# Fourth neighbour by SyncE or TensorE, and one in 42 history runs fetched by SyncE, in a recommender kernel

## The chip, the cores and the metric

The kernel runs on one core of a Trainium2 chip. The metric is the device time of one execution, in microseconds. The engines are named as in the profile: PE is TensorE, PEld its weight loads, DVE is VectorE, ACT is ScalarE, POOL is GpSimd and SP is SyncE. A letter q behind a name (SPq, ACTq) means the engine's sequencer, which runs register loads, waits and DMA issues.

## The reference

There are 50,001 items. Each has a row of 32 numbers in `E_in`, one in `E_out`, one of 64 numbers in `E_hist` and `E_tgt`, and a list of 32 neighbouring items. There are 16,384 users, each with 100 history items and one target item.

```python
def _neighbor_attn(E, near_full):            # for E_in (a_sus) and E_out (a_inf)
    V = E[near_full]                         # 32 neighbour rows per item
    scores = einsum('nd,nkd->nk', E, V) / sqrt(32)
    w = softmax(scores, axis=-1)
    return einsum('nk,nkd->nd', w, V)
h = concat([E_hist[history], a_sus[history], a_inf[history]])   # 100 rows of 128 per user
t = concat([E_tgt[target],  a_inf[target],  a_sus[target]])     # 1 row of 128 per user
x = h * t[:, None, :]
z = relu(x @ W1.T + b1)
scores = z @ W2[0]
exp_A = exp(scores) * ((history != target[:, None]) & (history != 0))
attn = exp_A / sum(exp_A) ** 0.5
s = sum(h * attn[..., None])                 # one number over all users
# then a cosine-like quotient of s and t per user, and a sigmoid
```

The cost is in two gathers of rows at random places: 32 neighbour rows for each item, then 100 item rows for each user.

## The kernel before

**Item stage.** The items are padded and cut into 23 blocks of 17 sub-blocks of 128 items, one item to a partition: 391 sub-blocks `s`. For each, a tile `v` of 128 x 32 x 64 numbers is filled with the neighbours' rows (`E_in` and `E_out` side by side, 256 bytes a row) from the input `egeo`. The 32 neighbours of a sub-block are fetched in three ways:

- Most by POOL: one indirect DMA (`nc.gpsimd.indirect_dma_start`, L215) fetches one neighbour of all 128 items.
- The last three (`NAUX` = 3) by ACT and DVE, with no DMA. `transposed` (L165 to L184) first puts the whole of `egeo` into SBUF, turned round, as `geoT`: one column of 128 numbers holds the rows of two items. `columns` (L222) loads 32 column addresses into an engine's registers (L189) and copies 32 single columns into a tile `g` (L229). `AUX` says which engine copies which quarter of which neighbour: six blocks of 32 on ACT and six on DVE. `turn` (L231) turns the `g` tiles back by TensorE, `even` (L238) writes the even item of each pair into `v`, and `odd_half` (L245) overwrites it where the odd one is wanted.
- The fourth last, in two of three sub-blocks (`SPNUM, SPDEN = 2, 3`), by SP: 128 single DMAs of 256 bytes from addresses in registers (L210), 32 addresses to one register load. In the third sub-block POOL fetches it.

The rest of an item is `products`, `scores`, `largest`, `exponents`, `weighted`, `attend`, `attended` and `finish`, on DVE and ACT. `finish` copies the result into two row buffers, `row` and `trow`, that ACT writes to the DRAM tensors `table` and `ttab` once in 17 sub-blocks. The order on PE, ACT, DVE and SP is written out by hand in the loop over `s` (L345 to L396): the stages of `s`, `s - 1`, `s - 2` and `s - 3` are interleaved. `v` has five buffers, so POOL and SP may be up to five sub-blocks ahead of the last reader of `v`. Ahead of the loop all 66 chunks of `geoT` are made at one go (L340).

**User stage.** The users are cut into 128 chunks `c` of 128, one user to a partition. The 100 history positions of a chunk make 13 groups `g`: twelve of eight positions and one of four. `gather` (L468) fetches each position of a group by one indirect DMA of POOL from `table` (L475, 512 bytes a row) into a tile `h`, of which there are six. `turn` (L484) transposes the eight 128 x 128 blocks (L490), multiplies by the target (L492) and sums rows (L495). `hidden` is the matrix product (L510) and relu (L511), `scored` the second product, one column per position (L519). `target_rows` (L429) fetches the target rows of a chunk with one more indirect DMA and, for every fourth chunk, has SP load the history numbers `hidx` (L433). The order within each engine is the scheduler's here.

A short last stage makes the sum over users and the output.

Of the kernel before, what the change touches and what calls it, by code (L numbers as in the profile page):

```python
# [18 lines left out]
P = 128  # L19
# [18 lines left out]
AUX = ("AAAA", "AADD", "DDDD",)  # L38
NAUX = len(AUX)
SPNUM, SPDEN = 2, 3  # L40
ENGINE = {"A": E.Activation, "D": E.DVE}
# [9 lines left out]
NG = L // LG  # L51


@with_exitstack
def kernel(
# [57 lines left out]
    with (  # L113
# [8 lines left out]
        tc.tile_pool(name="n_pt", bufs=3, space=bass.MemoryType.PSUM) as n_pt,  # L122
    ):
# [4 lines left out]
        def load(it):  # L128
# [4 lines left out]
            row = n_in.tile([P, NSUB, D], F32, name="row")  # L133
            nc.sync.dma_start(row[:, :, 0:DE], ehist_v[it])
            trow = n_in.tile([P, NSUB, 2 * G], F32, name="trow")
# [16 lines left out]
            nc.vector.tensor_copy(colf[:, :, 0:1], nidx[:, :, K - NAUX - 1 : K - NAUX])  # L152
# [10 lines left out]
            its[it] = (nidx, own, row, trow, odd, cols)  # L163

        def transposed(q):  # L165
# [10 lines left out]
            for n0 in range(0, n, 4):  # L176
                m = min(4, n - n0)
                ps = n_pt.tile([P, 4, P], F32, name="pt")
                for r in range(m):
                    nc.tensor.transpose(ps[:, r, 0:h], st[0:h, n0 + r, :], ident[0:h, 0:h])  # L180
                if (n0 // 4) % 2:
                    nc.vector.tensor_copy(into[:, n0 : n0 + m, :], ps[:, 0:m, 0:h])
                else:
                    nc.scalar.copy(into[:, n0 : n0 + m, :], ps[:, 0:m, 0:h])  # L184

        def registers(s, a, engine, i0, low, top):
# [3 lines left out]
                its[it][5][r : r + 1, i0 : i0 + NREG],  # L190
# [6 lines left out]

        def gather(s):
# [3 lines left out]
            g = [n_g.tile([P, P], F32, name=f"g{a}") for a in range(NAUX)]  # L202
            subs[s] = {"v": v, "g": g}
            k1 = K - NAUX - 1
            by_sp = s * SPNUM % SPDEN < SPNUM
            if by_sp:
# [7 lines left out]
            for k in range(k1 if by_sp else k1 + 1):  # L214
# [7 lines left out]
        def columns(s, a, i0):  # L222
# [3 lines left out]
            g = subs[s]["g"][a].bitcast(U8)  # L226
            copy = nc.scalar.copy if e == "A" else nc.vector.tensor_copy
            for i in range(i0, i0 + NREG):
                copy(g[:, 4 * i : 4 * i + 4], geoT_b[:, ds(vals[i - i0] - geoT_at, 4)])  # L229

        def turn(s):  # L231
            back = n_pt.tile([P, 4, P], F32, name="pt")
            for a in range(NAUX):
                nc.tensor.transpose(back[:, a, :], subs[s]["g"][a], ident)  # L234
            subs[s]["back"] = back
            subs[s]["aux"] = subs[s]["v"][:, K - NAUX : K].rearrange("p k t d -> p k (t d)")

        def even(s):  # L238
            it, j = divmod(s, NSUB)
            nc.scalar.copy(subs[s]["aux"], subs[s]["back"][:, 0:NAUX, 0 : 2 * G])  # L240
# [4 lines left out]
        def odd_half(s):  # L245
            it, j = divmod(s, NSUB)
            nc.vector.copy_predicated(
                subs[s]["aux"],
                its[it][4][:, j, :]
                .rearrange("p (a o) -> p a o", o=1)  # L250
                .to_broadcast([P, NAUX, 2 * G]),
                subs[s]["back"][:, 0:NAUX, 2 * G : 4 * G],
# [72 lines left out]
        def finish(s):  # L325
            it, j = divmod(s, NSUB)
            _, _, row, trow, _, _ = its[it]
            for t in range(2):
                nc.scalar.copy(
                    trow[:, j, t * G : (t + 1) * G], row[:, j, D - (t + 1) * G : D - t * G]  # L330
                )
            if j == NSUB - 1:
                nc.scalar.dma_start(table_v[it], row)
                nc.scalar.dma_start(ttab_v[it][:, :, DE:D], trow)
# [5 lines left out]
        for q in range(-(-PAIRS // (NST * P))):  # L340
            transposed(q)
        blocks = [(a, i0) for a in range(NAUX) for i0 in range(0, P, NREG)]
        acts = [(a, i0) for a, i0 in blocks if AUX[a][i0 // NREG] == "A"]
        dves = [(a, i0) for a, i0 in blocks if AUX[a][i0 // NREG] == "D"]
        for s in range(NT + 3):  # L345
            if s < NT:
                if s % NSUB == NSUB // 2 and s // NSUB + 1 < NITER:
                    load(s // NSUB + 1)
                gather(s)
# [3 lines left out]
            def act(i):  # L353
                if now and i < len(acts):
                    columns(s, *acts[i])

            def dve(i):
                if now and i < len(dves):
# [5 lines left out]
            if one:  # L364
                turn(s - 1)
# [269 lines left out]
```

## Time and profile before

| | |
|---|---|
| Time of the runs shown | 45,601.21 us median of 3 (45,563.7 to 45,709.14) |
| Profiled execution, its own time | 30,160.56 us |
| Span of the profile | 30,158.8 us |
| Item stage, first to last gather of POOL | 9.0 to 13,973.8 us |
| User stage, first to last gather of POOL | 14,001.6 to 30,140.0 us |
| Indirect DMAs by POOL | 11,078 (L215), 12,800 (L475), 128 (target rows) |
| Single-row DMAs by SP (L210) | 33,408 |
| Single-column copies by ACT and by DVE (L229) | 75,072 each |
| Mean granted PE clock | 0.799 (1.00 in the item stage, some 0.62 in the user stage) |

The profiled execution took about two thirds of the median of the timed runs. The profile does not show why.

How to read the page: part 1 gives the busy time of each engine. Part 2 cuts the span into 40 slices of 754 us, with one digit for the busy tenths of each. Part 4 follows the chain of work that ended last. Part 5 lists groups of instructions, with busy time and the mean ns of one, then the idle time ahead of them and what ended it. In the list of waits a line reads: who waited (engine, tile, line) <- for whom: total us, times, longest.

### The profile page before, as it was taken

To read this page: it belongs to the slowest core of one execution; us is meant where nothing else is said; L and a number is where in the kernel's file an instruction comes from. 1 tells how busy PE (TensorE), PEld (TensorE's weight loads), DVE (VectorE), ACT (ScalarE), POOL (GpSimd) and SP (SyncE) were. 2 spreads that over 40 slices of the span, in tenths; PEclk is the share of its full clock that TensorE was granted. 3 is DMA by queue.
4 is the path that set the end of the run, shared out by engine and by line. 5 is a ranking of instruction groups with operands and counts; after the bars stand their busy time and mean duration, and the time that the engine had idled before them with its cause. 6 is when DMAs were issued, how large, how long until landed. Compare 5 with 4: busy or idle time off the path is not lost.

```text
span 30158.8 us, 370867 instructions
## 1 busy us (share of the span) xinstructions
PE 13513.8 (45%) x46323; PEld 7666.4 (25%) x46323; DVE 13913.7 (46%) x83509; ACT 10305.2 (34%) x81987; POOL 22658.7 (75%) x24012
## 2 busy tenths in 40 slices
PE   1000000000000000003787787887887877878877
PEld 0000000000000000001444454444444444444444
DVE  5677777777777777775222222222222222222222
ACT  5565555555555555553111111111111111111111
POOL 6777777777777777777777777777777777777777
PEclk9999999999999999998656656666666666566566
DMA  2111111111111111111111111111111111111111
GB/s 62 31 36 32 32 34 34 32 32 34 34 32 32 34 34 32 32 34 40 54 53 54 53 54 53 54 53 54 53 54 53 54 53 54 53 54 53 54 53 52
DMA packets 1013118, 1347.05 MB, mean 45 GB/s; under 512 B 604800, under 2 KB 617664, under 8 KB 1007648
## 3 DMA queue, kind: packets, MB, share of 16 engines
q0 software_dynamic: 768192, 1211.79, 15.2%
q1 hardware_dynamic: 138480, 60.23, 0.8%
q10 hardware_dynamic: 103920, 51.31, 0.6%
q14 instruction: 2155, 17.65, 0.2%
q8 instruction: 371, 6.08, 0.1%
HBM read 1283.13 MB, written 51.30 MB: 44 GB/s over the span
## 4 chain that ended last, share of the span: by engine, by line
POOL 36%; issue 18%; DMA 16%; SPq 15%; PE 6%; DVE 4%; DVEq 0%; POOLq 0%; ACT 0%; ACTq 0%
POOL h L475 24%; DMA h<-table,hidx 13%; SPq L210 12%; POOL v L215 12%; PE z_ps L510 3%; SPq L189 3%; DMA v<-in_egeo_dram,nidx 2%; DVE g L229 1%; PE score L519 1%; PE hT_ps L490 1%; DVE xT L492 1%; DVE sc L268 0%; DVE prod L258 0%; DVEq L189 0%; DMA v<-in_egeo_dram 0%
## 5 line engine op out<-in xcount | busy, mean ns | idle before, releaser
L475 POOL DMA_INDIRECT h<-table,hidx x12800 | 12079.0, 944 | 3900.8 <-issue 3290.5
L215 POOL DMA_INDIRECT v<-in_egeo_dram,nidx x11078 | 10458.2, 944 | 3515.2 <-issue 3221.9
L229 ACT COPY g<-geoT 128x4 uint8 x75072 | 7377.3, 189 | 3385.9 <-issue 2729.6
L492 DVE TENSOR_TENSOR xT<-hT_ps,tT 128x1024 f32<-128x1024 f32 (+1 forms) x1664 | 1969.1, 1183 | 10939.1 <-PE hT_ps L490 10938.9
L511 ACT ACTIVATE z<-z_ps,b_sb 128x512 f32<-128x512 f32 x3200 | 2201.3, 688 | 12759.8 <-PE z_ps L510 12744.8
L490 PE MATMUL hT_ps<-ident,h 128*128 128x128 f32 x12800 | 5082.2, 414 | 3211.3 <-DMA h<-table,hidx 3001.2
L229 DVE COPY g<-geoT 128x4 uint8 x75072 | 5877.5, 197 | 808.2 <-issue 688.4
L234 PE MATMUL pt<-ident,g 128*128 128x128 f32 x1173 | 543.7, 471 | 12496.1 <-ACT g L229 10195.4
L510 PE MATMUL z_ps<-xT,w1T 128*128 128x512 f32 x6400 | 5806.6, 1009 | 24.7 <-DVE xT L492 24.6
L490 PEld LDWEIGHTS hT_ps<-ident,h 128*128 128x128 f32 x12800 | 2427.2, 193 | 8549.1 <-DMA h<-table,hidx 7900.2
L519 PEld LDWEIGHTS score<-w_sb,z 128*128 128x128 f32 x25600 | 4299.8, 253 | 0.6 <-issue 0.6
L519 PE MATMUL score<-w_sb,z 128*128 128x1 f32 x25600 | 3991.2, 278 | 0.0
L234 PEld LDWEIGHTS pt<-ident,g 128*128 128x128 f32 x1173 | 213.3, 184 | 12822.0 <-ACT g L229 10467.5
L258 DVE TENSOR_TENSOR prod<-v,own_ps 128x2048 f32<-128x2048 f32 x391 | 894.8, 2288 | 2684.3 <-DMA v<-in_egeo_dram 1470.5
L495 DVE TENSOR_REDUCE hsum<-h 128x8 f32<-128x1024 f32 (+1 forms) x1664 | 1943.4, 1168 | 0.0
L510 PEld LDWEIGHTS z_ps<-xT,w1T 128*128 128x128 f32 x6400 | 1886.8, 354 | 112.9 <-issue 70.3
L298 DVE TENSOR_TENSOR wv<-v,ex 128x1024 f32<-128x1024 f32 x782 | 1463.7, 1872 | 0.0
L268 DVE TENSOR_REDUCE sc<-prod 128x64 f32<-128x2048 f32 x391 | 889.7, 2275 | 0.0
L311 DVE TENSOR_REDUCE att<-wv 128x64 f32<-128x2048 f32 x391 | 883.7, 2260 | 0.1
L285 ACT ACTIVATE ex<-sc,top 128x32 f32<-128x32 f32 x782 | 227.0, 290 | 1343.5 <-DVE top L277 1330.8
L526 DVE TENSOR_TENSOR ea<-ea,keep 128x100 f32<-128x100 f32 x128 | 33.9, 265 | 1171.2 <-ACT ea L525 1171.2
L240 ACT COPY v<-pt 128x192 f32<-128x192 f32 x391 | 123.8, 317 | 1135.4 <-PE pt L234 1135.4
(67 smaller groups left out, 1585.7 us busy)
## 6 DMA issues: line engine op xcount, KB each, us to landing
v<-in_egeo_dram SPq DMA_DIRECT2D x33408, 0.2 KB
h<-table,hidx POOLq DMA_INDIRECT x12800
v<-in_egeo_dram,nidx POOLq DMA_INDIRECT x11078
table<-row ACTq DMA_DIRECT2D x23, 1088.0 KB
own<-in_egeo_dram SPq DMA_DIRECT2D x23, 544.0 KB
row<-in_ehist_dram SPq DMA_DIRECT2D x23, 544.0 KB
ttab<-trow ACTq DMA_DIRECT2D x23, 544.0 KB
ttab<-in_etgt_dram ACTq DMA_DIRECT2D x1, 12500.0 KB
```

The lines of the kernel that those rows point to most:

```text
L189: _, vals = nc.values_load_multi_w_load_instructions(its[it][5][r : r + 1, i0 : i0 + NREG], engines=[engine], min_val=low, max_val=top, sk ...
L210: nc.sync.dma_start(v[i0 + i : i0 + i + 1, k1].rearrange("p t d -> p (t d)").bitcast(U8), egeo_b[:, ds(vals[i], 8 * G)],)
L215: nc.gpsimd.indirect_dma_start(out=v[:, k].rearrange("p t d -> p (t d)"), out_offset=None, in_=egeo, in_offset=bass.IndirectOffsetOnAxis(a ...
L229: copy(g[:, 4 * i : 4 * i + 4], geoT_b[:, ds(vals[i - i0] - geoT_at, 4)])
L298: nc.vector.tensor_tensor(subs[s]["wv"][:, t].rearrange("p d k -> p k d"), subs[s]["v"][:, :, t, :], subs[s]["ex"][0][:, t, :] .rearrange( ...
L475: nc.gpsimd.indirect_dma_start(out=h[:, q, :], out_offset=None, in_=table, in_offset=bass.IndirectOffsetOnAxis(ap=u["hidx"][:, l : l + 1], ...
L490: nc.tensor.transpose(hT_ps[:, q, :], h[:, q, :], ident)
L492: x = nc.vector.tensor_tensor(xT[:, 0:w, :], hT_ps[:, 0:w, :], u["tT"].to_broadcast([D, w, P]), ALU.mult)
L495: s = nc.vector.tensor_reduce(u["hsum"][:, g * LW : g * LW + w], h[:, 0:w, :], AX.X, ALU.add)
L510: nc.tensor.matmul(z_ps, w1T, xT[:, q : q + LG, :], start=True, stop=True)
L511: nc.scalar.activation(z[:, q : q + LG, :], z_ps, AF.Relu, bias=b1_sb)
L519: nc.tensor.matmul(u["score"][:, l : l + 1], z[:, q, :], w2_sb, start=True, stop=True)
```

## The change

Item stage:

- `AUX` has a fourth entry ahead of the other three, "PPPP": four neighbours instead of three and two thirds are fetched without POOL, in every sub-block from the seventh on. `CYCLE = "PSSPS"` says who fetches the fourth: SP as before (S, 231 sub-blocks), or TensorE (P, 154). In a P sub-block `by_tensor` loads 128 addresses into PE's registers, 32 at a time, and makes 128 products of the identity with one column of `geoT`, which put the columns into a PSUM tile `pc` (one buffer). It runs in two halves of 64, one in the iteration before the sub-block's own and one in it. `evict` has ACT copy `pc` to SBUF, and `turn`, `even` and `odd_half` then treat four neighbours instead of three.
- The first six sub-blocks (`NFIRST`) have all 32 neighbours fetched by POOL. The 66 chunks of `geoT` are made during them, two at each of ACT's six places in an iteration, and all their evictions are by ACT.
- `trow` is gone. `row` is 160 numbers wide, one copy in `finish` repeats one half behind the other, and both DRAM writes read from it.

User stage:

- Of 768 runs of sixteen positions (two groups), every 42nd is fetched by SP: 18 runs. `one_by_one` has DVE make byte offsets `hoff`, and for each of 128 users SP loads 16 offsets into registers and issues 16 DMAs of 512 bytes into a tile `hs`, of which there are two. The first two runs are issued at the start of the stage, and run i + 2 where run i is used.
- The history numbers are loaded four blocks ahead (`AHEAD`), in `history_of`, from six buffers.

```diff
-AUX = ("AAAA", "AADD", "DDDD",)
+AUX = ("PPPP", "AAAA", "AADD", "DDDD")
-SPNUM, SPDEN = 2, 3
+CYCLE = "PSSPS"
+NFIRST = 6
+UG = 2
+UNIT = 42
+AHEAD = 4
...
+        tc.tile_pool(name="n_pc", bufs=1, space=bass.MemoryType.PSUM) as n_pc,
...
+        def kind(s):
+            return "" if s < NFIRST else CYCLE[s % len(CYCLE)]
...
-            by_sp = s * SPNUM % SPDEN < SPNUM
-            if by_sp:
+            if kind(s) == "S":
...
-            for k in range(k1 if by_sp else k1 + 1):
+            for k in range(k1 if kind(s) else K):
                 nc.gpsimd.indirect_dma_start(
...
             for i in range(i0, i0 + NREG):
-                copy(g[:, 4 * i : 4 * i + 4], geoT_b[:, ds(vals[i - i0] - geoT_at, 4)])
+                column = geoT_b[:, ds(vals[i - i0] - geoT_at, 4)]
+                if e == "P":
+                    nc.tensor.matmul(
+                        g[:, i : i + 1], ident, column.bitcast(F32), start=True, stop=True
+                    )
+                else:
+                    copy = nc.scalar.copy if e == "A" else nc.vector.tensor_copy
+                    copy(g.bitcast(U8)[:, 4 * i : 4 * i + 4], column)
+
+        def by_tensor(s, half):
+            if s >= NT or kind(s) != "P":
+                return
+            if half == 0:
+                subs[s] = {"g": [None] * NAUX}
+                subs[s]["g"][0] = n_pc.tile([P, P], F32, name="pc")
+            for i0 in range(half * P // 2, (half + 1) * P // 2, NREG):
+                columns(s, 0, i0)
+
+        def evict(s):
+            if kind(s) == "P":
+                g = n_g.tile([P, P], F32, name="g0")
+                nc.scalar.copy(g, subs[s]["g"][0])
+                subs[s]["g"][0] = g
...
             act(0)
             for i in range(5, len(dves)):
                 dve(i)
             if one:
+                evict(s - 1)
                 turn(s - 1)
                 even(s - 1)
                 odd_half(s - 1)
                 products(s - 1)
+            by_tensor(s, 1)
+            by_tensor(s + 1, 0)
             dve(0)
...
+        def one_by_one(c, g):
+            hs = u_hs.tile([P, UG * LW, D], F32, name="hs")
+            hoff = u_hs.tile([P, UG * LW], I32, name="hoff")
+            nc.vector.tensor_scalar(
+                hoff,
+                hists[c // BSUB][:, c % BSUB, g * LW : (g + UG) * LW],
+                9, None, ALU.logical_shift_left,
+            )
+            for p in range(P):
+                _, vals = nc.values_load_multi_w_load_instructions(
+                    hoff[p : p + 1, :], engines=[E.SP], min_val=0,
+                    max_val=(ITEMS - 1) * 4 * D,
+                    skip_runtime_bounds_check_because="worked out from an item's number",
+                )
+                for q in range(UG * LW):
+                    nc.sync.dma_start(
+                        hs[p : p + 1, q, :].bitcast(U8), table_b[:, ds(vals[q], 4 * D)]
+                    )
+            for i in range(UG):
+                early[c, g + i] = hs[:, i * LW : (i + 1) * LW, :]
...
+        units = [(c, g) for c in range(UC) for g in range(0, NW - UG + 1, UG)]
+        units = units[UNIT - 1 :: UNIT]
+        for i in range(AHEAD):
+            history_of(i)
+        for unit in units[:2]:
+            one_by_one(*unit)
         target_rows(0)
         for s in range(len(groups) + 2):
+            if s % (BSUB * NW) == 0 and AHEAD + s // (BSUB * NW) < UC // BSUB:
+                history_of(AHEAD + s // (BSUB * NW))
+            if s < len(groups) and groups[s] in units[:-2]:
+                one_by_one(*units[units.index(groups[s]) + 2])
```

## The prediction

> **What bounds the kernel now.** I read the table of stages first, one stretch from the middle of each stage.
>
> ```profile
> 2000.00:12000.00 10000.00, 396.30 (x866) 156.55 (x866) 7184.07 (x57215) 5751.46 (x56561) 7557.91 (x8007) 1.00 0.14 33
> 16000.00:26000.00 10000.00, 7988.57 (x27834) 4590.90 (x27835) 2459.69 (x2701) 1429.32 (x2301) 7558.89 (x8011) 0.62 0.19 53
> ```
>
> The columns are PE, PEld, DVE, ACT and POOL busy us, each with its count, then PE clock, DMA share and GB/s. POOL issues 8,007 and 8,011 instructions in 10,000 us: one every 1.249 us in both stages, though it looks only 76% busy. The groups say what the other 24% is.
>
> ```profile
> L475 POOL DMA_INDIRECT h<-table,hidx x12800 | 12079.0, 944 | 3900.8 <-issue 3290.5 <-DMA h<-table,hidx 328.2 <-PE z_ps L510 203.9
> L215 POOL DMA_INDIRECT v<-in_egeo_dram,nidx x11078 | 10458.2, 944 | 3515.2 <-issue 3221.9 <-DMA v<-in_egeo_dram 163.3 <-DMA v<-in_egeo_dram,nidx 65.9
> ```
>
> Each gather takes 0.944 us, and 0.305 us between two belongs to no one ("issue"). So POOL is full, and its count sets the time: 24,006 x 1.249 = 29,983 us of 30,158.8. What is left is 155 us of real gaps, by POOL's waits: 76.4 us at 185 us and 46.1 us at 905 us (below), 8 us at 331 us, and 28 us at the change of stage.
>
> ```profile
> POOL v L215 <- DMA v<-in_egeo_dram: 76.4, 1, 76.4
> ```
>
> ```profile
> POOL v L215 <- DVE wv L298: 46.1, 1, 46.1
> ```
>
> Then SP, which the busy table does not count: its register loads, a run of 32 DMAs in the timeline, and its waits.
>
> ```profile
> L189 SPq TENSOR_LOAD <-cols x1044: 2027/2176/2426, 168.9 to 13903.7; - x174
> ```
>
> ```profile
> 8015.12 10.58 SPq L210 DMA_DIRECT2D v<-in_egeo_dram  x32
> ```
>
> ```profile
> SPq L210 <- DVE wv L298: 233.2, 77, 4.5
> ```
>
> Min/median/max ns of one load of 32 registers, then 32 DMAs in 10.58 us, 0.331 us each. One sub-block by SP costs 4 x (10.58 + 2.18 + 0.1) = 51.5 us, so 261 of them are 13.4 ms of the 13.75 ms that SP's item work lasts: SP is nearly full too. In the user stage it has nothing to do but 32 loads.
>
> **What the Trainium skill says.** "Perfetto Trace Analysis", section "DMA Instruction — SWDGE (GPSIMD)": the profiler's end of a POOL DMA is the end of descriptor making, not of the move. The trace agrees: the DMA engines are 19% busy while POOL is full, so fewer POOL instructions, not fewer bytes, save time. "DMA: Bandwidth & Descriptors", section "Issuing engines are not separate DMA queues": issuing from another engine saves only sequencer time; here that is the scarce thing. On register loads the pages differ: "Runtime: NRT & Kernel Launch", section "Instruction fetch mechanics", gives about 200 ns per register from HBM, while the DMA page's section "Latency and other measured facts" gives a floor of about 600 ns. The trace has 2.18 us for 32 from SBUF, 68 ns each; it holds no load of another size.
>
> **The change, part by part.**
>
> *POOL's count.* Item stage: 385 sub-blocks x 28 + 6 x 32 = 10,972 instead of 11,078. User stage: 18 x 16 = 288 fewer. Together 394 x 1.249 = 492 us less. Both stages are POOL's, so this comes off the end, if every other path stays shorter.
>
> *The start.* In the kernel before, POOL stops at 185 us because SP's and ACT's neighbours of the first sub-blocks wait for `geoT`, made at one go, and SP starts its first gather only at 171 us and is behind; the gap at 905 us is DVE waiting for ACT's table write, which waits for a DMA of SP still under way. In the new order the first six sub-blocks need neither, and from then on SP has slack. I count the three gaps as gone: 76 + 8 + 47 + rounding = 127 us. The 28 us at the change of stage stay. A new wait could take this back; bounds 0 and 127.
>
> *SP in the item stage.* 231 x 51.5 = 11.9 ms against POOL's 10,972 x 1.249 = 13.7 ms. At most two S sub-blocks stand together (103 us against 70), which five `v` buffers cover. Cost nothing.
>
> *TensorE in the item stage.* Per P sub-block four register loads and 128 products, in halves of 64 that stand in PE's order between two `turn`s. Each product is a weight load, a matmul of one column, and a fused register instruction of four operations (one a division) that I see in the built program and that no row of the trace prices. Nearest rows: the 128x1 products of L519 run eight in 0.95 us at full clock (0.12 each); SP's 29 ns register move with its gap is some 60 ns. "TensorE: Matmul & The Clock Gate", section "Wait — 56ns, not 53.3ns?", has 62 ns of sequencer time per matmul. Lower bound 0.12 us, upper 0.12 + 4 x 0.06 + 0.06 = 0.42 us; I take 0.30. A half is 64 x 0.30 + 2 x 2.1 + 2 for the transposes = 25 us, in an iteration of 28 x 1.249 = 35.0 us. PE was 4% busy there. Behind it waits `turn`, and behind that ACT's `even` and DVE's products; they are late only above 0.45 us a product, and PE becomes the bound above (35.0 x 5 / 4 - 2.5 - 4.2)/64 = 0.58 us, since four of five iterations hold a half. Cost nothing.
>
> *ACT and DVE.* The same twelve column blocks as before; per P sub-block one eviction (0.3 us, as L240's 317 ns) and a third more in `even` and `odd_half`; one copy of 0.21 us fewer everywhere. DVE waits some 2.0 ms of the 10 ms in the stretch above for gathers, ACT some 2.2 ms for others: that covers them. The table write becomes 2,176 pieces of 512 bytes in place of 128 of 8,704; `ttab` has such pieces already and its issue takes 0.54 us. Nothing.
>
> *SP in the user stage* is the open term. A run is 2,048 x 0.331 = 677 us of DMAs and 128 loads of 16 registers. In DVE's built order `hoff` of run i + 1 stands right behind the second product of run i, so SP starts a run when the one before has been used: one at a time, not two (only the first two start together). Its cycle has about 10 us more: landing (2.4 us for a gather in the chain), sixteen transposes at 0.4 us, 1.2 us on DVE. POOL needs 7 chunks x 101 - 16 = 691 gathers x 1.249 = 863 us between two runs. The load of 16 decides:
> - in proportion to registers, 1.09 us (+0.1): cycle 677 + 152 + 10 = 839 us. Free.
> - a floor of 0.6 and the rest in proportion, 1.39 us: 878 us, 15 us late in each of 17 cycles, 255 us.
> - as long as 32 registers, 2.18 us: 979 us, 116 late, 17 x 116 = 1,970 us.
>
> I take 1.24, the middle of the first two: 859 us, just in time; for small delays I leave 20 us. DMAs of 512 bytes might issue more slowly than of 256: 0.331 is issue time, so I add none, and the third bound holds that too. History loads queue behind SP's runs, but four blocks ahead (16 chunks against 14).
>
> *Sum.* 492 + 127 - 20 = some 600 us off 30,160.6: 29,560 us, 2.0%. The median of the runs shown is 1.512 times the profiled execution, and no view shows why. If all durations are longer, the gain is 600 x 1.512 = 907 us (44,690 us); if it is a constant, 600 us (45,000 us). POOL's constant pitch in both stages speaks for a factor more than for a constant; I forecast 44,750 us.
>
> **Rivals.**
> 1. *SP becomes the bound of the user stage* (ends slower). Loads that cost nearly the same for 16 as for 32. For: SP, ACT and DVE all need 2.0 to 2.2 us, like a latency. Against: 68 ns a register, and a page that prices by register. It decides from a cycle of 863 + 619/17 = 899 us (1.63 us a load). At 2.18 us: 30,160 - 619 + 1,970 = 31,510 us, so 46,950 (constant) to 47,640 us (factor). Chance 0.14.
> 2. *PE becomes the bound of the item stage.* A fused register instruction of half a microsecond. At 0.8 us a product five iterations take 4 x 57.4 + 2 = 232 us instead of 175: 385 x 11.4 = 4.4 ms more, 33,930 us, so 49,400 (constant) to 51,300 us (factor). For: an unknown instruction. Against: every register instruction seen is below 60 ns. Chance 0.06.
> 3. *Part of the gain is eaten*: a load between 1.36 and 1.63 us, or the start gaps come back elsewhere. 100 to 600 us of profiled time lost: 45,000 to 45,600 us. Chance 0.17; a third of it ends within 0.3%.
> 4. *The change doesn't do what it says*: it does; the built program has 23,612 POOL gathers. What fails is "two runs under way", costed above.
>
> **How the numbers follow.** The forecast has 0.63. 0.3% (137 us, about the spread of the three runs) is the least that a measurement can tell from no change. Faster: 0.63 and two thirds of rival 3, 0.75; same 0.05; slower: rivals 1 and 2, 0.20. The range goes from 44,550 (all 619 us, times 1.512, and a little more) to 45,700 us, past rival 3, leaving out rivals 1 and 2. The likeliest case alone is 44,600 to 45,050 us.
>
> **What would show it.** Right: POOL keeps 1.249 us in both stages with 23,612 gathers; no POOL gap over 20 us before 1,000 us; SP's load of 16 below 1.36 us and SP waiting for DVE between runs; PE's products 0.45 us or less apart. Wrong: PE's transposes waiting for the SP DMAs of `hs` and POOL stopping behind full `h` buffers (rival 1); ACT's `even` waiting for PE most of an iteration and POOL waiting for `v` (rival 2).

## The result, and the profile after

The changed kernel takes 49,461.62 us (median of four runs, 49,444.41 to 49,472.13), the kernel before 45,608.41 us (45,563.7 to 45,709.14) beside it: 1.084 times the time, with a 95% interval of 1.082 to 1.086. It is slower by 3.85 ms where 0.85 ms less was forecast.

One thing has to be known to read the numbers. The same program runs in one of two ways from one occasion to another: the kernel before takes 30,160 to 30,164 us or 45,246 to 45,834 us. In the second way the other engines are held up while POOL gathers (shown below). The profile of before that the prediction read was taken in the first way; the runs that give the result, of both kernels, were made in the second. I call the two **free** and **held up**; kernels are compared within one of them only.

So the profile after, which is held up, has to be laid beside a held-up profile of the kernel before (experiment `e13_before`). That one comes from another session, in which the kernel before took 45,351 us at the median in place of 45,608, so the two profiles can be compared to within about 0.4 ms; the two halves of the change, measured in one session with `e13_before`, follow below. First the page of the changed kernel: its span, the busy time of each engine and the two groups of gathers.

```profile
span 49468.4 us, 534709 instructions
...
PE 19873.2 (40%) x85883; PEld 16304.9 (33%) x85883; DVE 15040.8 (30%) x82369; ACT 11095.9 (22%) x80592; POOL 22333.5 (45%) x23618
...
L550 POOL DMA_INDIRECT h<-table,hidx x12512 | 11834.2, 946 | 9054.4 <-issue 6279.3
...
L223 POOL DMA_INDIRECT v<-in_egeo_dram,nidx x10972 | 10377.5, 946 | 13673.5 <-DVE wv L332 10386.3
```

One gather takes 0.946 us (0.944 in the profile before), and there are 10,972 + 12,512 of them, as the prediction counted. But POOL is busy 45% of the span where it was 75%: it stands and waits. The table of two stretches of 10 ms, one in each stage, first of the changed kernel, then of the kernel before, both held up (PE, PEld, DVE, ACT, POOL busy us with counts, PE clock, DMA share, GB/s):

```profile
2000.00:12000.00 10000.00, 3720.10 (x17044) 3652.34 (x17044) 4603.25 (x32621) 3667.52 (x32141) 4263.76 (x4508) 1.00 0.10 19
30000.00:40000.00 10000.00, 4336.36 (x17806) 2995.04 (x17806) 1572.78 (x1733) 902.69 (x1470) 4745.24 (x5018) 0.61 0.14 34
```

```profile
2000.00:12000.00 10000.00, 220.88 (x482) 86.91 (x482) 4477.88 (x31794) 3515.07 (x31452) 4222.58 (x4465) 1.00 0.10 18
30000.00:40000.00 10000.00, 5128.61 (x22258) 3470.18 (x22259) 1967.82 (x2161) 1131.42 (x1841) 6060.64 (x6409) 0.65 0.17 43
```

Neither kernel makes 8,007 gathers in 10 ms here, as the free profile had it. In the item stage POOL makes 4,508 gathers in place of 4,465 in the same time, and each sub-block needs fewer. In the user stage it loses a fifth: 5,018 against 6,409. By the first and last gather of each stage: item stage 24,905 us before and 24,042 us after, user stage 20,149 and 25,250 us. The loss is all in the user stage, +5.1 ms, and 0.9 ms of it is won back in the item stage; which part of the item change wins it, where POOL is not what sets the pace (below), is not shown. The waits of PE and then of POOL, in the changed kernel, say where:

```profile
PE hT_ps L565 <- DMA hs<-table: 4300.2, 21, 253.4
```

```profile
POOL v L223 <- DVE wv L332: 10386.3, 382, 90.8
POOL h L550 <- issue: 6279.3, 11922, 11.0
POOL t L479 <- ACT z L586: 4207.9, 17, 261.8
```

At each of the 18 runs by SP, PE stands 223 to 253 us before the transposes of a tile `hs` that SP has not filled yet, 4.3 ms in all; behind it ACT's `z` is late, and POOL stands with all six `h` full, 17 times (4.2 ms) before its next target row and once, 241 us, before an `h`. That is the picture that the prediction described for rival 1 (PE's transposes waiting for the SP DMAs of `hs`). The first line of POOL's waits was there before as well, in the held-up kernel before:

```profile
POOL v L215 <- DVE wv L298: 10903.1, 382, 95.9
```

There POOL waits for DVE in 382 of 391 sub-blocks: POOL does not set the pace of the item stage at all in this way of running. The profile that was read ahead of the prediction had two such waits, 53 us in all.

### The profile page after: what moved, and what is told of

The parts are those of the page before. It is cut to its first block, busy times and chain, and to the rows that moved or that the text cites. A ratio compares the mean times of both kernels' runs of the same rounds, so it can differ in the third digit from the quotient of the medians.

```text
span 49468.4 us, 534709 instructions
## 1 busy us (share of the span) xinstructions
PE 19873.2 (40%) x85883; PEld 16304.9 (33%) x85883; DVE 15040.8 (30%) x82369; ACT 11095.9 (22%) x80592; POOL 22333.5 (45%) x23618
## 3 DMA queue, kind: packets, MB, share of 16 engines
q14 instruction: 2659, 21.78, 0.1%
## 5 line engine op out<-in xcount | busy, mean ns | idle before, releaser
L550 POOL DMA_INDIRECT h<-table,hidx x12512 | 11834.2, 946 | 9054.4 <-issue 6279.3
L243 ACT COPY g<-geoT 128x4 uint8 x73920 | 8227.8, 190 | 14317.9 <-issue 12456.1
L243 DVE COPY g<-geoT 128x4 uint8 x73920 | 6839.6, 177 | 10639.8 <-issue 10632.2
L238 PE MATMUL pc<-geoT,ident 128*128 x39424 | 8423.8, 348 | 2270.1 <-issue 2269.3
L238 PEld LDWEIGHTS pc<-geoT,ident 128*128 128x128 f32 x39424 | 8496.1, 332 | 2123.5 <-issue 2121.8
L594 PE MATMUL score<-w_sb,z 128*128 128x1 f32 x25600 | 4240.9, 286 | 6299.9 <-ACT z L586 4504.5
L585 PE MATMUL z_ps<-xT,w1T 128*128 128x512 f32 x6400 | 5064.2, 892 | 3445.0 <-DVE xT L567 2628.1
L565 PE MATMUL hT_ps<-ident,h 128*128 128x128 f32 x12512 | 3127.3, 351 | 318.4 <-issue 197.2
L585 PEld LDWEIGHTS z_ps<-xT,w1T 128*128 128x128 f32 x6400 | 1457.2, 277 | 4021.5 <-DVE xT L567 2815.7
L479 POOL DMA_INDIRECT t<-ttab,tidx x128 | 121.0, 946 | 4360.9 <-ACT z L586 4207.9
```

The lines of the kernel that those rows point to most:

```text
L238: nc.tensor.matmul(g[:, i : i + 1], ident, column.bitcast(F32), start=True, stop=True)
L243: copy(g.bitcast(U8)[:, 4 * i : 4 * i + 4], column)
L550: nc.gpsimd.indirect_dma_start(out=h[:, q, :], out_offset=None, in_=table, in_offset=bass.IndirectOffsetOnAxis(ap=u["hidx"][:, l : l + 1], ...
L565: nc.tensor.transpose(hT_ps[:, q, :], h[:, q, :], ident)
L585: nc.tensor.matmul(z_ps, w1T, xT[:, q : q + LG, :], start=True, stop=True)
L594: nc.tensor.matmul(u["score"][:, l : l + 1], z[:, q, :], w2_sb, start=True, stop=True)
```

## What holds the other engines up

This stretch of the timeline of the changed kernel shows ACT's copies of single columns (start, duration, and in brackets the idle time ahead of it) while POOL is gathering at 1.25 us each:

```profile
10025.14 0.19 ACT L243 COPY g<-geoT 128x4 uint8 x1 [1.21 <-issue]
10026.54 0.19 ACT L243 COPY g<-geoT 128x4 uint8 x1 [1.21 <-issue]
10027.94 0.19 ACT L243 COPY g<-geoT 128x4 uint8 x1 [1.21 <-issue]
10029.34 0.19 ACT L243 COPY g<-geoT 128x4 uint8 x1 [1.21 <-issue]
```

One copy every 1.40 us, and each is released by nothing but "issue": there is no wait on another engine. POOL's last gather before a pause starts at 10,042.5 us. The same table of counts for 16 us before and 5 us after that:

```profile
10024.00:10040.00 16.00, 0.33 (x2) 0.58 (x2) 2.44 (x12) 2.12 (x11) 12.04 (x14) 1.00 0.15 27
10053.00:10058.00 5.00, 0.00 (x0) 0.00 (x0) 4.91 (x36) 3.96 (x41) 0.00 (x0) 1.00 0.00 1
```

With POOL gathering (14 in 16 us), DVE and ACT each do less than one instruction per microsecond; with POOL at rest, 36 and 41 in 5 us. SP is hit in the same way. Its single-row DMAs of the user stage in one line each, of the changed kernel held up and then of the same kernel free (experiment `e18_after`):

```profile
30000.03 11.34 SPq L533 DMA_DIRECT2D hs<-table  x9
```

```profile
16000.44 9.71 SPq L533 DMA_DIRECT2D hs<-table  x26
```

Nine DMAs in 11.3 us against 26 in 9.7 us. This is **theory A**, which the experiments below test: held up, each sequencer other than POOL's gets about one instruction out per 1.4 us while POOL gathers without a pause; POOL then has to wait for them, its pauses let them catch up, and a stage's length is set by the number of instructions of the fullest other engine. The rivals were the **scaling reading**, that the measured time is the free time scaled by a factor or lengthened by a constant (the prediction's reading), and the **unseen-cost reading**, that one of the change's unseen costs (the load of 16 registers, the fused register instruction) is large, as in the prediction's rivals 1 and 2. The letters B to I in the recorded expectations stand for what each expectation says beside them. Three of them are taken up below: B (`e1_before`: only the new instructions of the change bring the slow stretches), D (`e5_after`: only the two halves of the change together bring them) and F (`e8_all_pool`: a cap on the rate of instructions of the whole core, POOL's gathers or not).

## The experiments

**The kernel before, again.** No edit.

> The kernel before, unchanged, profiled again. Its profile of 30,160 us and its timed median of 45,608 us differ by half, while the changed kernel's profile and median agree (49,468 and 49,462 us). Theory A (while POOL makes descriptors for a run of gathers without a pause, the other sequencers finish only one instruction in about 1.4 us each, as in the profile of the changed kernel; the shown profile of before fell outside this condition): span about 45,600 us, POOL between gathers some 65% of the span instead of 99%, DVE and ACT copies 0.7 or 1.4 us apart while POOL runs. Rival B (only the new instructions of the change, PE's fused register operations and SP's single-row DMAs, bring the slow stretches; the time of before is longer than its profile by something outside the span): span about 30,160 us again, no copy gaps of 0.7 or 1.4 us, POOL 99%.

30,163.6 us, span 30,161.8 us: free, as the profile shown ahead of the prediction. So that profile was no accident of profiling; the times of 45.6 ms are the other way of running.

**One half of the change at a time, free.** `e2_item_only` keeps the item part, `e3_user_only` the user part with the item stage of before.

```diff
-        units = units[UNIT - 1 :: UNIT]
+        units = []                        # e2_item_only
...
-AUX = ("PPPP", "AAAA", "AADD", "DDDD")    # e3_user_only: the item stage of before
-CYCLE = "PSSPS"
+AUX = ("AAAA", "AADD", "DDDD",)
+SPNUM, SPDEN = 2, 3
```

> The changed kernel without the 18 runs by SP in the user stage (units empty): the item part of the change alone. Theory A: item stage 24.05 ms as in the changed kernel, user stage that of before in the slow condition (some 23 ms), about 47,000 us; the item part costs 1,000 to 2,000 us because PE gets 128 x 3 instructions more in each P sub-block and needs POOL's pauses for them. Rival B: PE's fused register operations make the item stage slow, the user stage becomes fast again (16.1 ms): about 40,200 us.

29,897.6 us, 265 us less than the 30,162.9 us of before. By the prediction's own steps the item part is worth 106 gathers x 1.249 + 127 us = 259 us. Theory A's 47,000 us did not come, since nothing was held up here, nor did rival B's 40,200: the new instructions of PE alone bring no slow stretches. The same goes for the two figures of the next run.

> The item stage of the kernel before and the user stage of the change (18 runs by SP): the user part alone. Theory A: about 48,000 us, some 2,300 us above before; SP's 4,200 instructions a run compete for POOL's pauses. Rival B: item stage 14.0 ms as in the shown profile, user stage 25.4 ms: about 39,400 us. The forecast's own rival (a load of 16 registers too slow) would show a run cycle of 979 us; the profile of the changed kernel has 1.25 us a load and a cycle of some 1,390 us.

30,035.5 us, 127 us less. SP's run, 2,048 DMAs and 128 loads, takes 850 us and starts every 875.5 us, where POOL's gathers between two runs take 863: some 12.5 us late each time. The unseen-cost reading falls here, since both unseen costs are in these two kernels and neither costs milliseconds. The wait list of `e3_user_only` shows what SP itself waits for between runs:

```profile
SPq L491 <- DVE hsum L536: 477.3, 16, 95.1
```

One wait of 95 us and fifteen of some 25 us: SP starts a run only after the one before has been used, so "two under way" does not come about.

**All 32 neighbours by POOL, free.** No columns, no `geoT`, no single-row DMAs, no runs by SP.

```diff
-NFIRST = 6
+NFIRST = 1000
...
-        chunks = list(range(-(-PAIRS // (NST * P))))
-        some = -(-len(chunks) // (6 * NFIRST))
+        chunks, some = [], 1
...
-        units = units[UNIT - 1 :: UNIT]
+        units = []
```

> The changed kernel with all 32 neighbours of every sub-block fetched by POOL: no column copies, no products, no single-row DMAs, no geoT (NFIRST 1000, no chunks), and no runs by SP in the user stage. POOL has 12,512 + 12,800 gathers, 1,306 more than before. Theory A: DVE and ACT have some ten instructions a sub-block left, which fit beside POOL even at 1.4 us each, so the item stage is POOL's: 12,512 x 1.251 = 15.7 ms, and the whole some 39,000 us, 15% faster than before with more gathers. Theory of the prediction (POOL's count sets the time): 1,306 x 1.249 = 1,630 us slower than before, 47,200 us. Rival B: 15.7 + 16.1 = 31,900 us in the span.

31,815.0 us, 1,652 us more: 1,434 more gathers (12,512 less 11,078; the expectation's 1,306 is a slip) x 1.249 = 1,791 us, less the start gaps. While free, POOL's count sets the time, as the prediction had it.

**The changed kernel and a version with two runs really under way, held up.** The load of the history numbers moves from SP's queue to ACT's, after which DVE can make `hoff` of the next run earlier.

```diff
-            tc.keep_in_program_order(nc.sync.dma_start(hidx, hist_v[i]))
+            tc.keep_in_program_order(nc.scalar.dma_start(hidx, hist_v[i]))
```

> The changed kernel, unchanged, beside before in the same session. In the last session before took 30,163 us, and the two halves of the change alone gained 265 us (item part) and 127 us (user part); in the session of the result before took 45,608 us. Theory C (the chip can be in a condition in which POOL's gathers hold up the other sequencers; the cost of the change comes from that condition alone): where before is at 30,160 us, the halves add up to about 29,770 us, 1.3% faster, and its trace has no copies 1.4 us apart; where before is at 45,600 us, 49,460 us again. Rival D (the two halves together bring the slow stretches, neither alone does): 49,460 us beside a before of 30,160 us.

49,743.85 us against 45,793.94: 1.086 (1.085 to 1.088).

> The changed kernel with the history numbers loaded from ACT's queue instead of SP's: in the built order DVE's hoff of run i + 2 then stands ahead of run i's use, so two runs really are under way. Theory E (each run's cycle is 875 us against POOL's 863 because SP starts a run only after the one before has been used): SP never waits for DVE's use of the run before, the 17 delays of 13 us are gone, some 230 us less than the changed kernel where before is at 30,160 us: about 29,540 us. Rival (SP's own issue, 2,048 DMAs and 128 loads, is what takes 875 us): no change. Where before is at 45,600 us: within 1% of the changed kernel.

53,482.08 us, 1.167 (1.165 to 1.169): a miss, and it points the same way. DVE's waits in `e6_hist_by_act`:

```profile
DVE hoff L517 <- SPq L525: 8012.8, 16, 601.2
```

The buffer of `hoff` comes free only when SP has loaded the run's last registers. SP has too much to issue, and asking it earlier only puts DVE, with every product of the user stage behind it, to wait some 500 us for it. SP now goes from run to run without a gap, but a run takes it 1,623 us in place of 1,381 (medians); why is not shown. Whether two runs under way would save the 230 us of the free way was not met, since no free run of this version came.

**Is it POOL's gathers that hold the others up?** Three versions, first free, then the same held up: the kernel before; all 32 by POOL, so that the other engines have hardly an instruction in the item stage; and the kernel before with neighbours 0 to 13 filled by one plain DMA of other rows in place of 14 gathers (this leaves out that part of the item computation).

```diff
+            nc.sync.dma_start(             # e9_half_gathers, e11_half_gathers
+                v[:, 0:14].rearrange("p k t d -> p k (t d)"),
+                egeo[0 : 14 * P, :].rearrange("(p k) d -> p k d", k=14),
+            )
-            for k in range(k1 if by_sp else k1 + 1):
+            for k in range(14, k1 if by_sp else k1 + 1):
```

> The kernel before, unchanged, to see its profile on a chip where it takes 45,600 to 45,800 us. Theory A (while POOL gathers without a pause, every other sequencer finishes one instruction in about 1.4 us): POOL pauses some 22 us in each sub-block and some 3 to 4 us in each group of the user stage, copies 0.7 or 1.4 us apart while it runs and 95 ns apart while it pauses; item stage some 22.5 ms, user stage some 23 ms. On a chip where before takes 30,160 us: as in the shown profile, nothing of this.

> All 32 neighbours by POOL, no geoT, no column copies, no products, no single-row DMAs, no runs by SP; it took 31,815 us beside a before of 30,163 us in an earlier session, POOL full throughout. On a chip where before takes some 45,700 us: theory A expects the item stage at POOL's 15.7 ms, since DVE and ACT have some ten instructions left a sub-block, and the user stage as in before (some 23 ms): some 39,000 us, 15% faster than before. Theory F (a cap on the whole core's rate of instructions, 8 to 11 in a us, POOL's gathers or not): 250,000 instructions fewer, some 30,000 us. Theory of the prediction (POOL's count): slower than before by 1,630 us.

> The kernel before with half of POOL's item gathers left out: neighbours 0 to 13 of every sub-block are filled by one plain DMA with other rows, so the output is not the reference's. POOL has 5,474 gathers fewer, all other engines the same instructions (SP one DMA more a sub-block). On a chip where before takes some 45,700 us: theory A expects the slow stretch of each sub-block to be halved, 18 us less in 391 sub-blocks, about 39,000 us. Theory F (a cap on instructions per us regardless of POOL): about 45,500 us. On a chip where before takes 30,160 us: SP's 34 us a sub-block bound, about 29,900 us.

These ran free: 30,159.9, 31,816.1 and 30,196.6 us. The third is a finding too: with 5,474 gathers fewer the item stage takes 13,880 us instead of 13,965. The other engines alone need nearly as long as POOL, which now waits for them; its waits in `e9_half_gathers`:

```profile
POOL v L219 <- DVE wv L302: 6800.5, 382, 89.5
```

> All 32 neighbours by POOL and no runs by SP, once more, because the two earlier sessions of this kernel were on chips where before takes 30,160 us. Where before takes some 45,700 us: theory A (POOL's gathers hold up the other sequencers, so what counts is how many instructions they have) expects POOL full in the item stage, 15.7 ms, and some 39,000 us in all; theory F (a cap on the core's rate of instructions) some 30,000 to 34,000 us; the prediction's theory 1,630 us more than before.

> The kernel before with neighbours 0 to 13 of every sub-block filled by one plain DMA with other rows instead of 14 gathers of POOL, so the output is not the reference's. Where before takes 30,160 us it took 30,197 us: POOL's count halved in the item stage and no gain, since SP's 128 single-row DMAs then bound. Where before takes some 45,700 us: theory A expects the slow stretch of each sub-block to be halved, about 39,000 us; theory F no change, about 45,500 us.

Held up, more gathers make the kernel faster: `e10_all_pool` takes 37,974.82 us against 45,710.41, 0.831 (0.829 to 0.833), although free it is the slower by 5.5%. The group line of its item stage:

```profile
L223 POOL DMA_INDIRECT v<-in_egeo_dram,nidx x12512 | 13348.6, 1067 | 4152.0 <-issue 4055.0 <-DMA v<-in_egeo_dram,nidx 88.9 <-DMA nidx<-in_near_dram 8.0
```

POOL waits for no other engine there; its item stage takes 17.5 ms for 32 gathers a sub-block against 24.9 ms for 28 to 29. It is not the 15.7 ms that was expected: a gather takes 1.067 us here and starts 1.40 us after the last one (means), where in the free `e4_all_pool` it starts 1.248 us after. So POOL is held up a little too, which theory A leaves out. And `e11_half_gathers` takes 39,494.12 us, 0.864 (0.862 to 0.867): the same instructions on the other engines as before, but POOL half idle, and the item stage falls from 24.9 to 18.9 ms. Both ways of parting the gathers from the other engines' instructions shorten it. The scaling reading cannot give these: no factor or constant turns 1.055 into 0.831. Theory F expected 45,500 us for `e11_half_gathers` and falls too. Nor is it the amount that the DMA engines move: they move more in the item stage of `e11_half_gathers`, 24 GB/s against 18 in `e13_before`, and the stage is still the shorter one. Whether it is POOL's making of the descriptors or the DMA engines' work on them that holds the others up, these runs do not part; nor do they show that the count of the fullest engine alone sets the length of a stage.

**The kernel before and after, held up, with whole traces.**

> The changed kernel, unchanged. On a chip where before takes 30,160 us: its halves alone gained 265 and 127 us there, so theory C expects 29,770 us and no copies 1.4 us apart; rival D (the halves together bring the slow stretches) 49,500 us. On a chip where before takes some 45,700 us: 49,500 to 49,750 us as before.

> The kernel before, unchanged, for its profile where it takes some 45,700 us. Theory A: item stage some 25.1 ms (45.7 less the user stage of 20.5 ms that the half-gathers kernel, with the same user stage, had there), POOL pausing in every sub-block, copies 0.7 or 1.4 us apart while it runs. If it takes 30,160 us here: the shown profile.

49,595.89 us (1.085, 1.082 to 1.088) and 45,245.54 us. From `e13_before` come the lines of before shown above. Counted in its trace within the item stage, ACT starts some 1.6 instructions per us while POOL gathers and 5.3 while it rests, DVE 2.1 and 4.8, SP 1.4 and 4.3; in the free `e2_item_only` ACT and DVE make 6.0 and 6.1 beside POOL's gathers. These means are above one in 1.4 us because the hold-up sets in only some 6 to 10 us after POOL restarts; from 16 us on each of the three starts 0.5 to 0.8 per us. The kernel before has none of the change's instructions and is held up within its span all the same, so rival B falls.

The same count in the user stage of the changed kernel: SP starts 4.9 instructions per us beside POOL's gathers in the free `e18_after`, 2.4 in the held-up profile after, and 4.8 there in POOL's long pauses.

**SP's share taken back.** Every 64th run by SP in place of every 42nd, so 12 runs in place of 18.

```diff
-UNIT = 42
-AHEAD = 4
+UNIT = 64
+AHEAD = 6
```

> The changed kernel with one run in 64 by SP instead of one in 42 (12 runs instead of 18, history loads six blocks ahead). Where before takes some 45,700 us SP needs 1,391 us a run, back to back, against 1,120 us that 42 runs take without it; 64 runs take 1,710 us. Theory H (the loss of the user stage is SP's run becoming the longest path): PE no longer waits for hs, user stage some 20.3 ms, item stage 24.1 ms as in the changed kernel, some 44,500 us, 2.5% faster than before. Rival I (SP's instructions take slots from PE whether late or not, so the loss goes with their number): two thirds of the 5.0 ms loss stay, user stage 23.8 ms, some 47,900 us. Where before takes 30,160 us: 265 us from the item part and 12 x 16 x 1.249 = 240 us from the user part, some 29,660 us.

44,829.44 us, 0.988 (0.987 to 0.990). PE's waits hold no line for `hs` any more; SP's run takes 1,558 us (median), and one starts every 1,737 us, so SP waits between runs. The user stage is 20,749 us: the loss of some 5 ms is gone, but so is any gain there (before: 20,149 us in `e13_before`); what makes this version faster is its item stage, 23,815 us. So nearly all of the loss was SP's lateness, not the presence of its DMAs. What SP's remaining runs cost elsewhere, up to 0.6 ms, is not broken down.

**One half at a time, held up.**

> The user part of the change alone. It took 30,035 us beside a before of 30,163 us. Where before takes some 45,700 us: the whole loss is here, user stage 25.5 ms (18 runs of 1,391 us) and an item stage of some 25.1 ms, some 50,650 us. Rival (the loss is in the item part's products): no more than 46,000 us.

50,078.91 us, 1.104 (1.102 to 1.106). PE's waits in `e15_user_only`:

```profile
PE hT_ps L531 <- DMA hs<-table: 4366.5, 20, 258.4
```

> The item part of the change alone. It took 29,898 us beside a before of 30,163 us. Where before takes some 45,700 us: item stage 24.1 ms as in the changed kernel, user stage 20.5 ms, some 44,600 us, 2.4% faster. Rival (the products' 39,000 instruction pairs cost there): 47,000 us or more.

44,288.48 us, 0.976 (0.974 to 0.979). The halves give +4.73 and -1.06 ms, together +3.67; the whole change gave +3.85 beside the result and +3.58 to +3.95 in three other sessions. By stages, within this one session: the user part takes the user stage from 20,149 to 24,932 us and leaves the item stage as it is (24,905 and 24,919 us); the item part takes the item stage to 23,868 us and the user stage to 20,325. The wait of 4.3 ms belongs to the user part alone. One half alone brings the loss, so rival D falls.

**The whole change, free.** Two more runs of the changed kernel were to meet the free way of running.

> The changed kernel once more, one look. If the other engines' instructions issue at full rate beside POOL's gathers here (the kernel before then at about 30,160 us), the gains of its halves add up: 30,162 - 265 - 127 = about 29,770 us. If they are held up (the kernel before then at 45,250 to 45,800 us), about 49,600 us again, ratio 1.085.

48,912.4 us against 45,335.7, a ratio of 1.079: held up again.

> The changed kernel once more, one look. If the other engines' instructions issue at full rate beside POOL's gathers here (the kernel before then at about 30,160 us), the gains of its halves add up: 30,162 - 265 - 127 = about 29,770 us. If they are held up (the kernel before then at 45,250 to 45,800 us), about 49,000 to 49,700 us again, ratio 1.08.

29,772.71 us against 30,161.14, a ratio of 0.987 (a single run of each): free, and within 3 us of the sum of the halves. The table of stages of `e18_after`:

```profile
2000.00:12000.00 10000.00, 6614.85 (x30210) 6411.51 (x30211) 7284.51 (x57891) 5811.51 (x57024) 7558.19 (x8007) 1.00 0.18 34
22000.00:28000.00 6000.00, 4657.60 (x16845) 2760.98 (x16845) 1489.76 (x1639) 864.69 (x1392) 4469.27 (x4735) 0.63 0.22 54
```

POOL makes 8,007 gathers in 10 ms of the item stage, as before, beside 30,210 matmuls of PE where there were 866 (each product is two of them, see below). In the user stage it makes 4,735 in 6 ms, which is one in 1.267 us: it loses a little. Its waits say that this is the one thing lost:

```profile
POOL t L479 <- ACT z L586: 219.3, 22, 13.5
```

The largest gap in the user stage is 13 us, against 262 us in the held-up run of the very same program.

## Why the prediction was wrong, point by point

The free run prices each term of the sum, the held-up runs the step that failed.

- **POOL's count.** 394 x 1.249 = 492 us. The counts and the pitch are exactly so in `e18_after`: 23,612 gathers at 1.249 us and 254 us of gaps make up its span. Right while free. Held up it is beside the point, since POOL waits.
- **The start.** Taken as 127 us, all gone (the three gaps, 76 + 8 + 47, make 131; `e2_item_only` gives 265 - 132 = 133). In `e18_after` POOL has no gap over 1.6 us before 13,712 us. The 28 us at the change of stage stayed. Right while free. Held up, POOL has pauses of some 20 to 50 us from 209 us on.
- **TensorE in the item stage.** Taken as 0.30 us a product between 0.12 and 0.42. In `e18_after` it is 0.427 us, above the upper bound (min/median/max ns):

```profile
L238 PE MATMUL pc<-geoT,ident x39424: 212/352/368, 275.3 to 13698.1; 128*128 x200
L238 PEldq FUSED_REGOPS  x19712: 81/85/103, 275.1 to 13694.1; - x200
```

  There are 19,712 products (154 x 128) and as many fused register instructions, but 39,424 matmuls: each fp32 product is two, each with its weight load, and they start 0.213 us apart when nothing holds PE up. The prediction read its nearest row by the same slip: L519 has 25,600 matmuls for 12,800 columns, so eight in 0.95 us are four products, 0.24 us each. The fused instruction takes 85 ns, not 240. No cost while free was right, but by a hair and by luck: the limit was 0.45 us. In the item stage held up, PE still cost nothing on balance: `e16_item_only` is faster.
- **SP's load of 16 registers.** Taken as 1.24 us between 1.09 and 2.18. In the profile after it is 1.246 us (min/median/max ns):

```profile
L525 SPq TENSOR_LOAD <-hoff x2304: 3/1246/1489, 24176.7 to 49168.5; - x192
```

  With 2.18 us for 32 that makes 0.058 us a register and 0.31 us for the rest. "Runtime: NRT & Kernel Launch", section "Instruction fetch mechanics", with its 200 ns a register from HBM, does not price a load from SBUF here. It is no longer held up than free (1.257 us in `e18_after`), so the load isn't what made SP late. Rival 1 named the right place and picture, by the wrong mechanism. Its limit of 1.63 us a load does not come out of the prediction's own terms, either: a cycle of 899 us leaves 1.56 us, (899 - 677 - 10) / 128 - 0.1.
- **SP's cycle in the user stage.** Taken as 849 us of run and 10 us of landing and turning, 859 us. Free, the run is 850 us, but 25.7 us pass between two runs: the term of 10 us is mis-sized. 875.5 us is 12.5 us over POOL's 863; the eighteen gaps sum to 226 us where 20 were left for small delays. "One at a time, not two" was right.
- **The sum.** 492 + 127 - 226 = 393 us, measured 388 (30,161.1 to 29,772.7). So in the free way the mechanism of the sum holds, and the 600 us were too many by that one term.
- **The step that failed** is the one from the profile to the median: "The median of the runs shown is 1.512 times the profiled execution, and no view shows why", with "POOL's constant pitch in both stages speaks for a factor more than for a constant". It is neither. The pitch was constant because that execution was free, and it says nothing of the one that was timed. Held up, the 0.331 us of an SP DMA do not hold: a run of SP takes 1,383 us in place of 850, and its cycle is 1,389 us, nearly back to back, 18 x 1,389 = 25.0 ms, which is the whole user stage. The interval on the other side does not grow as much: 42 of 768 runs of the 20,149 us of `e13_before` are 1,102 us in place of 863. So SP, taken as 4 us short of POOL's interval, is late by well over 200 us each time (PE's 223 to 253 us above). At 1.512 times, its 859 us would have been 1,299 us and POOL's 863 us 1,305; a single factor keeps their order, and this is what hid the loss.
- **The range** reached to 45,700 us and left out rival 1 as a matter of the load's length alone. A median half as long again as the profile, with no view that shows why, should have been an unknown cost with ends of its own: any duration of any engine could have been the one that grew.

## What to carry to other kernels

Compare the time of the profiled execution with the median first; where they differ by more than their spread, the profile may describe another way of running than the one that is measured. Here no sum from it carried over by a factor. Work that is moved off the bound to an engine "with nothing to do" has to be priced per instruction on that engine, with slack: here 4,200 sequencer instructions a run were given 0.5% of slack, and a slower issue turned a gain of 1.3% into a loss of 8%. Taking fewer runs (64 in place of 42) or the item part alone was faster than the kernel before by 1.2% and 2.4% held up, and the item part by 0.9% free as well (a single run; 64 was not run free). For held-up running alone, the fewest instructions beside POOL (all 32 neighbours by POOL, 0.831) is best of the whole computations tried.

## What the runs showed of the hardware that was not expected

- While POOL issues indirect DMAs every 1.25 us, the other sequencers may be held to about one instruction in 1.4 us; a register move of SP, 29 ns at its median, took up to 1.42 us. POOL's own gathers stay at 0.946 us beside them in the kernels before and after, but in `e10_all_pool`, where POOL does not pause, they start 1.40 us apart on average. The hold-up begins some 6 to 10 us after POOL starts. In the item stage it ends for ACT, DVE and SP together, some 4.5 us after the end of POOL's last gather; in the user stage SP is free again some 3 us after it. One plain consequence is that a kernel with more gathers and fewer other instructions (`e10_all_pool`) is 17% faster there and 5.5% slower free.
- An fp32 matmul that is no transpose stands in these traces as two, each with its own weight load (39,424 for 19,712 products at L238). Counts of matmuls have to be halved before a price per product is taken from them.
- What puts a run into the one way or the other stays open. The PE clock is 1.00 in the item stage in both ways and 0.61 and 0.63 in the user stage (tables of the changed kernel above), so it isn't that clock; the programs are the same, with 534,709 instructions in both profiles of it. The seven sessions of the experiments were on seven chips, by the numbers on record, and all runs of a session went the same way: free on chips 4, 13 and 14, held up on 3, 5, 8 and 15. That would fit something about the chip, but each chip was met once, so chip and occasion are not parted.
- Nor is it shown what the sequencers lack while they are held up. That it is the fetching of instructions would fit "issue", but the transfers that fetch them are no slower: the changed kernel has the same 2,659 and 759 packets in its two instruction queues both ways, with medians of 455 and 1,092 ns held up and 448 and 1,080 ns free. They bring 34.2 MB for 534,709 instructions, 64 bytes each, so a packet of 8,192 bytes would be some 128 instructions, while the hold-up falls on single ones. A wait between the arrival of a packet and the issue, or for something else, is not seen in the traces.
